# First and last groups of a two-layer graph network: statistics behind the adjacency transpose, split copies, row scalings and a tail on VectorE, and store deadlines taken from products

## The chip, the cores and the metric

The kernel runs on one core of a Trainium2 chip. Five instruction queues work side by side: TensorE (PE) for matrix products, VectorE (DVE), ScalarE (ACT), GpSimd (POOL), and SyncE (SP), which only issues DMAs here. The metric is device microseconds of one execution. The time is a median of three runs; one further execution was profiled.

## The reference

There are 128 batches, each of 128 tokens of width 512. Layer 0 mixes the tokens with the 128 x 128 adjacency matrix, adds the result to its input and normalises; layer 1 is masked attention with 8 heads of width 64, a projection, an inner layer norm, the residual and an outer layer norm.

```python
def layer0(x):                            # W1 = W2 = adj
    A = einsum('od,bdn->bon', adj, x); C = A + b[None, :, None]
    pre = A[:, :, None, :] + (C - A)[:, :, :, None]
    return layernorm(x + max(relu(pre), axis=-1))      # no gamma, no beta
def layer1(x):
    q, k, v = heads(x @ w_qkv)
    attn = softmax(where(mask == 0, -inf, q k^T * hd**-0.5))
    o = (attn @ v) @ w_proj + b_proj
    ln = layernorm(o) * gamma + beta
    return layernorm(x + o + ln)
```

The mask is built from `adj`. The maximum over the last axis needs only a row maximum of `A` and the bias, so layer 0 is one product with `adj` for each batch, a row maximum, and a norm.

## The kernel before

**Staging.** The 128 batches go in 32 groups of G = 4. All arithmetic is float32. Loop step `p` of the main part works on several groups at once: attention output of group p-1 (`attend`), scores and softmax of group p (`scores`, `softmax`), values of group p (`v_unit`), the layer-0 product of group p+2 (`l0_mm`) and its norm and transposition (`group_l0`), output projection of group p-1 (`o_unit`), queries and keys of group p+1 (`token_sums`, `qk_unit`), and the final norms and stores of group p-1 (`tails`). A prologue does layer 0 of groups 0 and 1 and the queries and keys of group 0 (`qk_plain`); an epilogue handles the last two groups batch by batch (`tail_pool`, `seed_last`, `project`, `tail_open`, `tail_close`, `outer`).

**Softmax** (L1020). For a batch, DVE adds the mask to the scores out of PSUM (`s<-k,mask`), takes row maxima (`nm<-s`), ACT makes eight exponentials with sums (L1054), DVE the reciprocals (`rec<-sm`), ACT scales the eight heads by them (L1071), and DVE transposes in 32 x 32 blocks (`pu<-s`, L1083). A pair of DMAs (`hop<-pu`, `s<-hop`) finishes the transposition through DRAM.

**Queries and keys** (`qk_unit`, L739). A fast-multiplication scheme has 26 nodes. A node is one or more products into a PSUM bank `k`; POOL's `hl` sums are their left sides. From some nodes ACT copies the bank to another bank that continues it (`seeds`, shown as `ACT k L773`) or to a snapshot in SBUF (`ACT u L777`). Two nodes in each group need a snapshot added to their bank by DVE before they go on (`k<-k,u`, L340): first node 7, then node 11. ACT then copies the second sum to `u`, and PE continues in that bank. The results leave through DVE (`qk<-k,u`).

**Final norms** (`tails`, L1155). For each half of a batch pair DVE runs two `scalar_tensor_tensor` operations through the helper at L343: `z<-o,mvo,ga_bc`, (o - mean) x gamma, and `z<-z,rs,o`, z x root + o. POOL adds the residual `xr`, ACT norms (L501), SP stores.

**Who sets the order.** The program calls `plan.add` with engine, cost, reads and writes. PE operations form a chain in program order. `Plan.schedule` (L217) lists all others: each operation gets a due time from its successors, and of those ready on an engine the most pressing goes first. Operations without successors, mainly stores, take a common due time at the end of everything:

```python
end = max(ideal[op] + op.cost for op in ideal) + 9.0
due = min((s.due - ... for s in op.succs), default=end)
```

`Plan.run` (L194) repeats this with shifted PE start times, four times (`ROUNDS`), and keeps the order that ends first. Each engine then executes its instructions in the order so found. Helpers record all operations of a kind, so many instructions have one line: L340 two-input elementwise, L343 `scalar_tensor_tensor`, L346 products, L350 DMAs.

**Prologue, lines that matter.** `l0_stats` (L516) calls `bn` (L457) for four batches; `finish` (L462) makes root and shift on POOL; `l0_transpose_pe` (L567) transposes on PE and copies 128x512 with one DVE instruction (L583); PE's order is l0 products for batches 0 to 3, transposes, `qk_plain(0)`, transposes, four `l0_mm`, `qk_plain(1)`.

**Epilogue, lines that matter.** For a batch of group 30, `tail_pool` (L1348) does inner statistics, a POOL finish of three small operations, an ACT norm, three POOL two-input operations (x gamma, + o, + residual) and `outer`. For a batch of group 31 `tail_open` (L1386) and `tail_close` (L1406) add the residual to the projection with an identity product on PE and read it from PSUM with a DVE `scalar_tensor_tensor`.

Of the kernel before, what the change touches and what calls it, by code (L numbers as in the profile page):

```python
# [135 lines left out]
class Op:  # L136
    __slots__ = ("n", "eng", "cost", "emit", "lag", "kb", "preds", "succs", "due", "start", "done")
# [22 lines left out]
class Plan:  # L160
# [5 lines left out]
    def add(self, eng, cost, emit, reads=(), writes=(), lag=None, kb=0):  # L166
        op = Op(len(self.ops), eng, cost, emit, self.LAG[eng] if lag is None else lag, kb)
        for accesses, writing in ((reads, False), (writes, True)):
            for a in accesses:
                buf, key = a if type(a) is tuple else (a, None)  # L170
                assert self.slots[buf.slot] is buf, buf.slot
                for other, k, w in buf.log:
                    if (w or writing) and (k is None or key is None or k == key):
                        op.preds.add(other)
                if buf.before is not None and (writing or not buf.log):
                    op.preds.update(o for o, _, _ in buf.before.log)
                buf.log.append((op, key, writing))
        if eng == "PE":
            if self.pe is not None:
                op.preds.add(self.pe)  # L180
            self.pe = op
        op.preds.discard(op)
        self.ops.append(op)
        return op
# [6 lines left out]
    ROUNDS, KEPT = 4, 0.5  # L191
    SLOWER, LATER = 1.05, 2.0

    def run(self, lead):  # L194
        for op in self.ops:
            for p in op.preds:
                p.succs.append(op)
        t = lead
        start = {}
        for op in self.ops:  # L200
            if op.eng == "PE":
                start[op] = t
                t += op.cost
        best = None
        for _ in range(self.ROUNDS):
            order = self.schedule(start)
            last = max(op.done for op in start)
            if best is None or last < best[0]:
                best = last, order
            t = was = lead  # L210
            for op in start:
                t += self.KEPT * (op.start - was)
                was, start[op] = op.done, t
                t += op.cost
        return best[1]

    def schedule(self, ideal):  # L217
        ops = self.ops
        end = max(ideal[op] + op.cost for op in ideal) + 9.0
        for op in reversed(ops):  # L220
            ahead = op.lag + (self.AHEAD_DMA + 1.5 * op.kb / self.KB_PER_US if op.kb else self.AHEAD)
            due = min(
                (s.due - (0.0 if s.eng == op.eng == "PE" else ahead) for s in op.succs),
                default=end,
            )
            if op in ideal:
                due = min(due, ideal[op] + op.cost)
            op.due = due - op.cost
# [56 lines left out]
def kernel(  # L285
# [137 lines left out]
    plan.add("DVE", 0.25, lambda: pin(V.tensor_copy(adjT.t, pt0.t[:, :P])), [pt0], [adjT])  # L423
# [33 lines left out]
    def bn(src, reads, mv, c):  # L457
        st = small("st", 6)
        plan.add("DVE", 0.61, lambda: pin(V.bn_stats(st.t, src())), reads, [st])  # L459
        plan.add("DVE", 0.09, lambda: pin(V.bn_aggr(mv.t[:, c], st.t)), [st], [(mv, c)])  # L460
# [33 lines left out]

    def norm(dst, src, stat, reads, writes):
        rs, sh, i = stat
        plan.add(
            "ACT",
            0.7,
            lambda: pin(  # L500
                A.activation(  # L501
                    dst(), src(), AF.Identity, bias=sh.t[:, i : i + 1], scale=rs.t[:, i : i + 1]
                )
            ),
            [rs, sh, *reads],
            writes,
        )
# [8 lines left out]
    def l0_stats(g):  # L516
        mv = buf(f"mvy{g % 2}", [P, G, 2])
        for j in range(G):
            xb = xs[2 * g + j // 2]
            bn(lambda xb=xb, j=j: xb.t[:, j % 2], [(xb, j % 2)], mv, j)  # L520
        return mv
# [45 lines left out]
    def l0_transpose_pe(f, k):  # L567
# [5 lines left out]
        def emit():  # L573
            for c in range(KC):
# [4 lines left out]
        plan.add(  # L579
            "DVE",  # L580
            0.61,
            lambda: pin(
                V.tensor_copy(  # L583
                    xT.t[:, h, :, ts(j, P)], b.t.rearrange("p (c n) -> p c n", c=KC)
                )
            ),
            [b],
            [(xT, (h, j))],
        )
# [97 lines left out]
    def qk_plain(h, banks, eng):  # L687

        xT = x1T_buf(0)
        for n in range(4):  # L690
            b = bank(banks[n])
            for half in range(2):
# [11 lines left out]
                plan.add("PE", 1.725, emit, [raw[n], (xT, (h, 0)), (xT, (h, 1))], [b])  # L704
# [315 lines left out]
    def softmax(b, bs):  # L1020
# [45 lines left out]
        for i in range(H):  # L1066
            plan.add(
                "ACT",
                0.295,
                lambda i=i: pin(  # L1070
                    A.activation(  # L1071
                        flat()[:, i], flat()[:, i], AF.Identity, scale=rec.t[:, i : i + 1]
                    )
                ),
                [rec, (s, i)],
                [(s, i)],
            )
        u = buf(f"pu{b % 2}", [P, Q, H, QS])
# [132 lines left out]
    for c in range(4):  # L1211
        (s,) = finish(mv0, [c], rcol[0])
        l0_norm_one(0, c, s)
# [4 lines left out]
    qk_plain(0, (0, 1, 2, 3), ("ACT", "DVE", "ACT", "DVE"))  # L1218
    for f in range(2, 4):
        l0_transpose_pe(f, 4 + f)  # L1220
    for f, k in zip(range(4, 8), (0, 1, 2, 3)):
        l0_mm(f, k)
# [4 lines left out]
    qk_plain(1, (4, 5, 6, 7), ("ACT", "DVE", "ACT", "DVE"))  # L1227
# [25 lines left out]
    for p in range(NG - 1):  # L1253
# [9 lines left out]
        for j in range(G):  # L1263
            softmax(a + j, bs[j])
# [48 lines left out]
    for j in range(G):  # L1313
        softmax(a + j, bs[j])
# [33 lines left out]
    def tail_pool(b, o, j):  # L1348
# [4 lines left out]
        (st,) = finish(mv, range(1))  # L1353
        norm(z, lambda: o.t[:, j], st, [o], [zk])
        for with_, op, rd in (
            (lambda: ga_bc.t, ALU.mult, ga_bc),
            (lambda: o.t[:, j], ALU.add, o),
            (r, ALU.add, rk),
        ):
            plan.add(  # L1360
                "POOL", 1.25, lambda with_=with_, op=op: tt(GP, z(), z(), with_(), op), [zk, rd], [zk]
            )
# [23 lines left out]
    def tail_open(b, pb):  # L1386
# [3 lines left out]
        rs = small("rs", G)  # L1390

        def root():
            pin(GP.tensor_scalar(rs.t[:, :1], mv.t[:, 0:1, 1], EPS, None, ALU.add))
            tt(GP, rs.t[:, :1], rs.t[:, :1], mhalf.t, ALU.pow)

        plan.add("POOL", 0.8, root, [mv, mhalf], [rs])
# [9 lines left out]
    def tail_close(b, pb, rs):  # L1406
# [3 lines left out]
        plan.add("PE", 0.862, lambda: mm(pb.t, ident.t, r(), False), [rk, ident], [pb])  # L1410
        plan.add(
            "DVE",
            0.65,
            lambda: stt(z(), z(), rs.t[:, :1], pb.t, ALU.mult, ALU.add),
            [zk, pb, rs],
# [8 lines left out]
    for j in range(G):  # L1424
        tail_pool(a - G + j, os_[g - 1, j // 2], j % 2)
    project(a, pbs[0])
    attend(a + 2, Y[0])
    opened = [tail_open(a, pbs[0])]
    project(a + 1, pbs[1])
    attend(a + 3, Y[1])  # L1430
    opened.append(tail_open(a + 1, pbs[1]))
    tail_close(a, pbs[0], opened[0])
    project(a + 2, pbs[2])
    opened.append(tail_open(a + 2, pbs[2]))
# [49 lines left out]
```

## Time and profile before

| what | value |
|---|---|
| median of 3 runs | 1915.88 us (1914.39 to 1916.46) |
| the profiled execution | 1916.16 us; its span 1914.4 us, so 1.76 us lie around the span |
| mean granted TensorE clock | 0.994 |
| busy PE / DVE / ACT / POOL | 98% / 81% / 73% / 70% |
| PE instructions' idle time put down to releasers, all waits | 18.8 us in 17 waits |
| PE busy from 0 to 50 / 50 to 100 us | 45.96 / 45.06 us |
| PE busy from 100 to 1840 us | 1733.57 of 1740 us |
| PE busy from 1840 to 1900 / 1900 to 1915 us | 51.80 / 0.00 us |

A row of the profile names engine, line and operation, then out<-in by the program's buffer names. Brackets at a timeline row give the idle time just before the instruction on its engine and what released it. PE's end times are modelled, so its busy share is an upper figure. The table says where PE isn't busy: the first 100 us, the last 75 us, and a little in between.

### The profile page before, as it was taken

Reading aid. Unit: us, or ns where it says so; the run is one execution under the profiler, and the core shown is the slowest. Engines: PE = TensorE matmul, PEld = TensorE weight load, DVE = VectorE, ACT = ScalarE, POOL = GpSimd, SP = SyncE. Lnnn points to the kernel's source line nnn. Section 1 sums busy time; section 2 is a strip of 40 time slices with the busy share of each in tenths; the row PEclk is TensorE's granted clock in tenths of the full one; section 3 lists DMA queues with packets and bytes.
Section 4 is the critical chain, followed back from the end, with each engine's and each line's share of the span. In section 5 each row is a group of like instructions: output and inputs, shape, how many; then the busy total and the mean of one; then the engine's idle time right before and its main releaser. Section 6 shows DMA issues by size and latency. Waiting matters only on the chain.

```text
span 1914.4 us, 35277 instructions
## 1 busy us (share of the span) xinstructions
PE 1876.4 (98%) x11307; PEld 1595.4 (83%) x11307; DVE 1558.2 (81%) x2634; ACT 1405.4 (73%) x4285; POOL 1332.8 (70%) x1454
## 2 busy tenths in 40 slices
PE   9899999999999999999999999999999999999995
PEld 6788888888888888888888888888888888888882
DVE  7678878889788878888788888888788887888774
ACT  2776778777778777778777787776788767787784
POOL 7658667667577767777677767686776776777746
PEclk9999999999999999999999999999999999999998
DMA  6656675566766566765576756676765667666653
GB/s 204 183 130 155 184 204 162 171 168 193 204 188 168 172 179 187 210 178 167 164 194 179 211 164 172 169 200 186 211 144 172 179 188 210 178 170 171 165 193 116
DMA packets 444856, 341.89 MB, mean 179 GB/s; under 512 B 276736, under 2 KB 378240, under 8 KB 444672
## 3 DMA queue, kind: packets, MB, share of 16 engines
q1 hardware_dynamic: 444384, 339.11, 63.7%
q8 instruction: 91, 1.49, 0.3%
q14 instruction: 93, 0.76, 0.1%
q10 hardware_dynamic: 288, 0.52, 0.1%
HBM read 172.82 MB, written 166.72 MB: 177 GB/s over the span
## 4 chain that ended last, share of the span: by engine, by line
PE 91%; DVE 3%; ACT 3%; POOL 1%; issue 1%; DMA 0%; ACTq 0%; DVEq 0%; POOLq 0%
PE k L346 91%; DVE z L343 2%; ACT s L1071 1%; ACT s L1054 1%; POOL x L340 1%; DVE wqk L340 0%; ACT u L777 0%; DVE k L340 0%; POOL rs L340 0%; ACT k L773 0%; DMA x<-in_x_dram 0%; DVE qk L343 0%; ACT x L501 0%; DVE st L459 0%; DVE x1T L583 0%
## 5 line engine op out<-in xcount | busy, mean ns | idle before, releaser
L346 PE MATMUL k<-hl,wqk 128*128 128x256 f32 x2232 | 518.9, 380 | 2.1 <-ACT k L773 2.0
L346 PEld LDWEIGHTS k<-hl,wqk 128*128 128x128 f32 x2232 | 424.4, 190 | 61.2 <-POOL hl L340 2.5
L1054 ACT ACTIVATE s<-s,nm 128x128 f32<-128x128 f32 x1024 | 397.2, 391 | 31.2 <-DVE nm L1045 31.2
L340 POOL TENSOR_TENSOR hl<-x1T 128x512 f32<-128x512 f32 (+1 forms) x250 | 237.8, 961 | 134.3 <-PE k L346 90.2
L1071 ACT ACTIVATE s<-s,rec 128x128 f32<-128x128 f32 x1024 | 325.5, 392 | 0.0
L346 PE MATMUL k<-x1T,wqk 128*128 128x256 f32 x992 | 250.0, 383 | 9.1 <-ACT u L777 5.6
L886 ACT COPY u<-k 128x512 f32<-128x512 f32 x189 | 110.0, 582 | 196.1 <-PE k L346 195.4
L777 ACT COPY u<-k 128x512 f32<-128x512 f32 x341 | 194.2, 584 | 73.2 <-DVE k L340 30.6
L346 PE MATMUL k<-wv,hl 128*128 128x256 f32 x1024 | 241.4, 379 | 0.0
L346 PEld LDWEIGHTS k<-wv,hl 128*128 128x128 f32 x1024 | 194.5, 190 | 52.1 <-issue 21.5
L346 PE MATMUL k<-wp,so 128*128 128x256 f32 x992 | 224.8, 379 | 0.5 <-ACT k L861 0.5
L343 DVE SCALAR_TENSOR_TENSOR s<-k,mask 128x512 f32<-128x512 f32 x256 | 156.2, 683 | 83.0 <-PE k L346 83.0
L346 PEld LDWEIGHTS k<-x1T,wqk 128*128 128x128 f32 x992 | 188.3, 191 | 40.6 <-ACT u L777 11.4
L343 DVE SCALAR_TENSOR_TENSOR qk<-k,u 128x512 f32<-128x512 f32 x248 | 165.4, 682 | 62.9 <-PE k L346 39.9
L346 PEld LDWEIGHTS k<-wp,so 128*128 128x128 f32 x992 | 188.4, 190 | 26.6 <-ACT k L861 0.9
L340 POOL TENSOR_TENSOR hl<-x1T,hl 128x512 f32<-128x512 f32 (+1 forms) x249 | 201.9, 822 | 0.5 <-DMA x1T<-xhop 0.5
L1054 ACT ACTIVATION_READ_ACCUMULATOR s<-s,nm 128x1 f32 x1024 | 194.2, 190 | 0.0
L346 PE MATMUL k<-wv,x1T 128*128 128x256 f32 x768 | 179.5, 383 | 0.0
L340 POOL TENSOR_TENSOR x<-x,be_bc 128x1024 f32<-128x1024 f32 x62 | 153.2, 2470 | 35.1 <-ACT xr L501 16.4
L346 PE MATMUL k<-wp,oT 128*128 128x256 f32 x744 | 170.7, 379 | 0.0
L1083 DVE STREAM_TRANSPOSE pu<-s 128x1024 f32<-128x1024 f32 x128 | 158.1, 1235 | 12.1 <-ACT s L1071 12.0
L1132 ACT COPY oT<-k 128x512 f32<-128x512 f32 x128 | 74.9, 585 | 120.3 <-PE k L346 120.3
(139 smaller groups left out, 3345.1 us busy)
## 6 DMA issues: line engine op xcount, KB each, us to landing
hop<-pu SPq DMA_DIRECT2D x128, 512.0 KB, 2.7
s<-hop SPq DMA_DIRECT2D x512, 128.0 KB, 3.7
spill<-x SPq DMA_DIRECT2D x62, 512.0 KB, 4.3
xhop<-xt SPq DMA_DIRECT2D x248, 128.0 KB, 3.4
x1T<-xhop SPq DMA_DIRECT2D x248, 128.0 KB, 5.0
x<-in_x_dram SPq DMA_DIRECT2D x60, 512.0 KB, 5.9
xr<-spill SPq DMA_DIRECT2D x60, 512.0 KB, 5.4
out_dram<-xr SPq DMA_DIRECT2D x60, 512.0 KB, 4.4
```

Source lines behind the costliest of these rows:

```text
L340: pin(eng.tensor_tensor(dst, a, b, op))
L343: pin(V.scalar_tensor_tensor(dst, a, s, b, op0, op1))
L346: pin(PE.matmul(dst, lhsT=lhsT, rhs=rhs, start=start, stop=True, skip_group_check=True))
L777: plan.add("ACT", 0.5, lambda b=b, u=u: pin(A.copy(u.t, b.t)), [b], [u])
L886: plan.add("ACT", 0.5, lambda: pin(A.copy(u.t, b.t)), [b], [u])
L1054: A.activation(flat()[:, i], flat()[:, i], AF.Exp, bias=nm.t[:, i : i + 1], accum_out=sm.t[:, i : i + 1],)
L1071: A.activation(flat()[:, i], flat()[:, i], AF.Identity, scale=rec.t[:, i : i + 1])
L1083: V.transpose(u.t.rearrange("p q h b -> p h q b"), flat().rearrange("p h (q a) -> p h q a", q=Q),)
L1132: lambda: pin(A.copy(dst.t[:, :, ts(jj, P)], bk.t.rearrange("p (c n) -> p c n", c=KC))),
```

## The change

1. **Statistics of group 0** are placed behind the copy of the transposed adjacency (`behind=[adj_done]`).
2. **`finish_first`**: for group 0, the shift is made by two small DVE operations; POOL keeps only the root.
3. **Split copies**: the 128x512 copy out of the PE transpose becomes two halves, the first on DVE, the second on ACT, and each half of a `qk_plain` product waits for its halves alone.
4. **Order on PE**: l0 products of batches 6 and 7 go between the second and third output block of `qk_plain(1)`.
5. **`softmax(on_vector)`**: for the four batches of group 0 and the first two of group 31, the eight ACT scalings become one DVE multiplication, 128x1024, with the reciprocals broadcast.
6. **Epilogue**: `tail_pool` becomes `tail_before`, called batch by batch between the attention and projection steps: the ACT norm and two of the three POOL operations become two DVE `scalar_tensor_tensor`s. `tail_close` loses its identity product; DVE adds the projection to the residual in SBUF and then combines. The shift of these inner norms is no longer needed, and `root_only` makes the roots.
7. **Planner**: an operation without successors takes its due time from the start of the PE operation that was the latest when it was added, plus 9.0 (`BEHIND`); six rounds instead of four; the starts of the best order are kept with it. PE's order in the main loop isn't touched by this, but the orders of DVE, ACT, POOL and SP are.

```diff
-    def add(self, eng, cost, emit, reads=(), writes=(), lag=None, kb=0):
+    def add(self, eng, cost, emit, reads=(), writes=(), lag=None, kb=0, behind=()):
         op = Op(len(self.ops), eng, cost, emit, self.LAG[eng] if lag is None else lag, kb)
+        op.after = self.pe
+        op.preds.update(behind)
...
-    ROUNDS, KEPT = 4, 0.5
+    ROUNDS, KEPT, BEHIND = 6, 0.5, 9.0
...
-                best = last, order
+                best = last, order, [op.start for op in order]
...
-        end = max(ideal[op] + op.cost for op in ideal) + 9.0
...
-            due = min(
-                (s.due - (0.0 if s.eng == op.eng == "PE" else ahead) for s in op.succs),
-                default=end,
-            )
+            if op.succs:
+                due = min(s.due - (0.0 if s.eng == op.eng == "PE" else ahead) for s in op.succs)
+            else:
+                due = ideal.get(op.after, 0.0) + self.BEHIND
...
+    def finish_first(mv, c, rows):
...
+        plan.add("POOL", 0.85, root, [(mv, c), mhalf], [rs])
+        plan.add("DVE", 0.12, lambda: tt(V, t..., mean, rows, ALU.add), ...)
+        plan.add("DVE", 0.12, lambda: stt(sh..., rows, t, rs, ALU.subtract, ALU.mult), ...)
...
-            bn(lambda xb=xb, j=j: xb.t[:, j % 2], [(xb, j % 2)], mv, j)
+            bn(lambda xb=xb, j=j: xb.t[:, j % 2], [(xb, j % 2)], mv, j, [adj_done])
...
+            if half:
+                plan.add("ACT", 0.4, lambda ops=operands: pin(A.copy(*ops())), [b], at)
+            else:
+                plan.add("DVE", 0.4, lambda ops=operands: pin(V.tensor_copy(*ops())), [b], at)
...
+        if on_vector:
             plan.add(
-                "ACT",
-                0.295,
...
+                "DVE",
+                1.55,
+                lambda: tt(
+                    V, flat(), flat(), rec.t.unsqueeze(2).to_broadcast([P, H, P]), ALU.mult
+                ),
...
-    for f, k in zip(range(4, 8), (0, 1, 2, 3)):
-        l0_mm(f, k)
+    for f in (4, 5):
+        l0_mm(f, f - 4)
...
-    qk_plain(1, (4, 5, 6, 7), ("ACT", "DVE", "ACT", "DVE"))
+    qk_plain(1, (4, 5, 6, 7), copies, range(2))
+    for f in (6, 7):
+        l0_mm(f, f - 4)
+    qk_plain(1, (4, 5, 6, 7), copies, range(2, 4))
...
-            softmax(a + j, bs[j])
+            softmax(a + j, bs[j], p == 0)
...
-        softmax(a + j, bs[j])
+        softmax(a + j, bs[j], j < 2)
...
-        (st,) = finish(mv, range(1))
-        norm(z, lambda: o.t[:, j], st, [o], [zk])
-        for with_, op, rd in (
-            (lambda: ga_bc.t, ALU.mult, ga_bc),
-            (lambda: o.t[:, j], ALU.add, o),
-            (r, ALU.add, rk),
-        ):
+        rs = root_only(mv, range(1))
+        plan.add("DVE", 0.7, lambda: stt(z(), o.t[:, j], mv.t[:, 0, 0:1], ga_bc.t, ALU.subtract, ALU.mult), ...)
+        plan.add("DVE", 0.7, lambda: stt(z(), z(), rs.t[:, :1], o.t[:, j], ALU.mult, ALU.add), ...)
+        plan.add("POOL", 1.25, lambda: tt(GP, z(), z(), r(), ALU.add), [zk, rk], [zk])
...
-        plan.add("PE", 0.862, lambda: mm(pb.t, ident.t, r(), False), [rk, ident], [pb])
+        plan.add("DVE", 0.65, lambda: tt(V, r(), r(), pb.t, ALU.add), [pb, rk], [rk])
...
-            lambda: stt(z(), z(), rs.t[:, :1], pb.t, ALU.mult, ALU.add),
+            lambda: stt(z(), z(), rs.t[:, :1], r(), ALU.mult, ALU.add),
...
-    for j in range(G):
-        tail_pool(a - G + j, os_[g - 1, j // 2], j % 2)
+    tail_before(a - 4)
     project(a, pbs[0])
     attend(a + 2, Y[0])
+    tail_before(a - 3)
```

## The prediction

> **What bounds the kernel now.** I read the page's slices and chain first, then PE's waits, then the timeline where those waits lie.
>
> ```profile
> PE   9899999999999999999999999999999999999995
> ACT  2776778777778777778777787776788767787784
> ...
> PE 91%; DVE 3%; ACT 3%; POOL 1%; issue 1%; DMA 0%; ACTq 0%; DVEq 0%; POOLq 0%
> ```
>
> PE is the chain; only the first slices and the last fall short. So whatever adds PE idle time adds that time, and other engines count only where PE waits for them or after its end. PE's waits say where that is:
>
> ```profile
> PE k L346 <- ACT u L777: 5.6, 5, 1.1
> PE k L346 <- ACT k L773: 5.1, 3, 3.1
> PE k L346 <- DMA s<-hop: 1.5, 1, 1.5
> PE k L346 <- DVE u L355: 1.2, 1, 1.2
> PE k L346 <- DVE adjT L423: 1.0, 1, 1.0
> ...
> PE k L346 <- DVE x1T L583: 0.9, 1, 0.9
> PE k L346 <- DVE z L343: 0.9, 1, 0.9
> PE k L346 <- DVE qk L712: 0.9, 1, 0.9
> ```
>
> By windows, adjT, x1T and qk L712 are the prologue, ACT k L773 is 4.8 us in 50 to 100 us (loop step 0), ACT u L777 is five stalls spread over the middle, DMA s<-hop is the tail. PE's last product ends at 1895.8 of 1914.4 us: 18.6 us of tail follow it.
>
> Step 0 in the timeline, PE at the ends of its two waits for seed copies:
>
> ```profile
> 82.79 1.10 PE L346 MATMUL k<-hl,wqk 128*128 128x256 f32 x4 [1.76 <-ACT k L773]
> ...
> 86.34 0.57 ACT L773 COPY k<-k 128x512 f32<-128x512 f32 x1
> ...
> 86.96 2.08 PE L346 MATMUL k<-x1T,wqk 128*128 128x256 f32 x4 [3.07 <-ACT k L773]
> ...
> 88.83 1.91 PE L346 MATMUL k<-hl,wqk 128*128 128x256 f32 x4
> ```
>
> The seed copies stand in ACT's queue behind 32 exponentials and 32 scalings, and after the second wait four matmuls take 2.08 us instead of 1.03: with 1.91 for 1.03 and the next eight (2.91 for 1.89) that is 2.9 us more.
>
> A middle stall, one of five:
>
> ```profile
> 260.14 0.70 DVE L340 TENSOR_TENSOR k<-k,u 128x512 f32<-128x512 f32 x1 [0.55 <-PE k L346]
> 260.75 1.88 DVE L343 SCALAR_TENSOR_TENSOR z<-o,mvo,ga_bc 128x512 f32<-128x512 f32 x1
> ...
> 262.55 3.44 DVE L343 SCALAR_TENSOR_TENSOR z<-z,rs,o 128x512 f32<-128x512 f32 x2
> ...
> 265.91 0.69 DVE L340 TENSOR_TENSOR k<-k,u 128x512 f32<-128x512 f32 x1
> ...
> 267.27 1.13 PE L346 MATMUL k<-x1T,wqk 128*128 128x256 f32 x4 [1.12 <-ACT u L777]
> ```
>
> Three z operations lie between the group's two DVE adds. The adds start d = 5.77 us apart; ACT's copy and PE follow the second by 1.36 us. Groups with two z's have d = 4.06 to 4.64 and no stall: **the stall is d - 4.64**.
>
> [...] a z takes 0.70 us alone, 1.7 to 2.85 beside POOL's 128x512 and 128x1024 sums; z<-z,rs,o averages 1.28. [...] doubled matmuls after 3.07 us of waiting, and pairs of l0 products at 2.07 us early on against 1.02 later. [...]
>
> **The change part by part**, against the profiled 1916.16 us.
>
> *Prologue.* (a) With the statistics behind it, the adjT copy no longer waits for a bn_stats that ended at 5.91 us; the transpose ended at 4.31. Of the 1.0 us wait and 0.3 us before, 0.1 to 1.0 can pass on, since the statistics (4 x 0.69) come later and the norms of batches 0 and 1, which bind the first transposes, follow DVE's order: 0.5. [...] Two DVE shift operations for three POOL ones: nothing, beside l0 products. (b) qk_plain(1) starts at 35.64 after waits of 0.86 (DVE qk L712, for a bank) and 0.90 (x1T copies, 34.31 to 35.58, late in DVE's queue behind wqk sums of 1.5 us which POOL blocks). With l0_mm of 6 and 7 moved behind two output blocks, the bank wait has 7 us of cover, and a half copy is 0.35 us on DVE with the other on ACT: of 1.76 us about 1.1 goes, what stays is the first DVE half behind a wqk sum. The moved l0_mm (4 x 0.5 us of PE) are neither added nor removed; their row maxima and norms come 7 us later, ahead of group 1's work by far more. Together -1.6 (-0.6 to -2.1).
>
> *Step 0.* 32 scalings leave ACT (pitch 0.305 us: 9.8 us), more than both waits, 1.76 + 3.07 = 4.8; with them go 2.9 us of slow clock: 7.7. Four DVE multiplications 128x1024 come: [...] DVE is busy 30.5 of 50 us there[...]. Queued behind them are the transposes pu (1.25 us), a DMA hop and two v adds; PE waits for those up to 1 us: **-7** (-8 to -4).
>
> *Planner.* Stores are due earlier now, so the final norms and z's before them are placed earlier. The compiled order keeps PE's instructions of the middle, but between the two adds DVE now has three z's in 9 groups (steps 2, 6, 9, 12, 15, 17, 20, 23, 26), xt and three z's in 7 (7, 10, 13, 18, 21, 24, 27), one z in 8, against three z's in 5 groups and two in most others before. Sixteen stalls instead of five. A group with one z can't give back: PE has no wait there. Each stall is at least what the trace has for three z's, 1.12; I take 1.12 for all 16, because the xt (0.70, one input, not blocked) runs while [...]z would stand anyway: 16 x 1.12 - 5.6 = **+12.3**. Upper end: laid against POOL's sums as traced, d is 5.99 and 6.31, stalls 1.35 and 1.67: 9 x 1.35 + 7 x 1.67 - 5.6 = +18.2; with one more blocked z, d = 6.9, up to +29. Lower end: the sums start at other times and the z's pass between them: -5.6, no stall. SP's queue carries stores earlier and loads as before; its DMA share is 0.65, so I take nothing, 0 to +2 if a reload is passed.
>
> *Tail.* ACT loses 16 scalings (4.9 us) in the last softmax, for two DVE multiplications[...]; so the exponentials, transposes and the DMA pair that PE waited for (1.5) come about 4 us earlier; 4 identity products (4 x 0.5 us) go from PE. After PE's end the chain was POOL: 1.26 us operations up to 1897.3, then roots; the last norm ended at 1911.5 and the span 2.9 later. Eight of twelve POOL operations (8 x 1.25 = 10 us) go, for 8 DVE ones at 0.70; four PSUM adds (0.65)[...] come too. DVE has about 25 us of work from the first attend on, and ends some 56 us after the last scores start (1840.9); roots 1.9, two norms 1.5 and 2.9 to the end make 62, against 73.5: **-11** (-6 to -14). If DVE's operations are blocked by the POOL adds left, -6.
>
> Sum: -1.6 - 7 + 12.3 - 11 = -7.3, or 1908.9 against 1916.16. The profiled run lies 0.28 above the median, so 1908.6, called 1909.
>
> **The rivals.**
> *The middle takes no harm.* POOL starts with PE's products, and its order changes too; if the z's fall between its sums, d stays under 4.64. Against it: three z's never did that in the five groups that had them. Sum -1.6 - 7 - 11 - 5.6 + up to 5: 1891 to 1896, say 1895. Chance 0.19.
> *The middle eats the gain, slower.* One mechanism: z's blocked by POOL's sums between the two adds, in 16 groups. The gains are 19.6 and the old stalls 5.6; it decides where a stall averages over 25.2 / 16 = 1.58 us, d over 6.2. For it: 5.99 and 6.31 from traced rows, and a longest z of 2.85. Against: the old 5.77. At d = 6.9 (2.26 each) +30.6 - 19.6 = +11: 1927; at 6.4, +3.4. Chance 0.27.
> *The tail is DVE's.* -6 instead of -11, and step 0 gives -5: -1.6 - 5 - 6 + 12.3, about 1916. For it: DVE is the fullest engine there after PE. Chance 0.16.
> That the planner change leaves the middle alone is excluded by the compiled order.
>
> **How the numbers follow.** The forecast has 0.38. A measurement of this kernel tells about 0.2%, 3.8 us, from no change. Faster takes the forecast but for 0.02, and the first rival: 0.55. Within: 0.02, the tail's 0.15 and 0.02 of the slow case: 0.19. Slower: 0.26. The forecast's own range is 1902 to 1912; with the others' inner halves 1896 to 1923.
>
> **What would show it.** Right: first l0 product near 5 us; no wait over 0.5 us near 34 us; ACT k L773 waits below 1 us in 50 to 100 us and no doubled matmuls at 87; PE <- ACT u L777 some 16 times, 1.1 each; last norm some 11 us nearer to the last scores. The forecast is wrong if ACT u L777 stays under 6 us in all (then near 1895), or passes 25 (then slower), or if the POOL roots in the tail still end over 10 us after PE.

## The result: 0.4% slower

The changed kernel takes 1923.66 us (median of 6 runs, 1920.72 to 1924.34), the kernel before 1915.14 in the six that stand beside them. The ratio is 1.0041, 95% interval 1.0028 to 1.0054. The forecast was 1909, with a range of 1896 to 1923. The profiled execution took 1924.27 us with a span of 1922.5, against 1916.16 and 1914.4.

The page of the changed kernel, chain by engine:

```profile
PE 84%; DVE 7%; ACT 5%; issue 2%; POOL 1%; DMA 1%; ACTq 0%; SPq 0%; DVEq 0%
```

PE's share of the chain fell from 91% to 84%: some of the time of others is now on the path. PE's three largest waits, by what ended them (total us, times, longest; the change moves lines, so L346 of before is L349, L773 is L810 and L777 is L814):

```profile
PE k L349 <- ACT u L814: 23.0, 16, 1.7
PE k L349 <- DVE x1T L625: 4.4, 2, 3.3
PE k L349 <- ACT k L810: 2.3, 3, 1.2
```

Sixteen stalls on `u`, as many as forecast, but 23.0 us in all instead of 18. Of the 4.4 us for x1T, 1.1 is the wait at the first queries and keys, which was 0.9 before; the 3.3 are new. The seed copies cost 1.2 us in step 0 instead of 4.8.

To put the 8.1 us of span in their place I cut each trace where PE starts the scores of a group (the `k<-qk` rows of the timeline). "Step 0" goes from the first group's scores to the second's, "middle" from there to the last group's, "tail" from the last group's to the end of the span.

| us | to first scores | step 0 | middle | tail |
|---|---|---|---|---|
| before | 49.65 | 54.28 | 1736.93 | 73.51 |
| changed | 52.58 | 47.55 | 1755.95 | 66.41 |
| difference | +2.9 | -6.7 | +19.0 | -7.1 |
| forecast | -1.6 | -7 | +12.3 | -11 |

**The middle.** The timeline of one of the seven groups with xt and three z's between the adds:

```profile
490.29 0.70 DVE L343 TENSOR_TENSOR k<-k,u 128x512 f32<-128x512 f32 x1 [1.05 <-ACT k L810]
490.89 0.70 DVE L570 STREAM_TRANSPOSE xt<-x 128x512 f32<-128x512 f32 x1
...
491.52 0.71 DVE L346 SCALAR_TENSOR_TENSOR z<-o,mvo,ga_bc 128x512 f32<-128x512 f32 x1
...
491.68 2.77 POOL L343 TENSOR_TENSOR x<-x,be_bc 128x1024 f32<-128x1024 f32 x1 [0.51 <-DVE xt L570]
492.14 4.53 DVE L346 SCALAR_TENSOR_TENSOR z<-z,rs,o 128x512 f32<-128x512 f32 x2
...
494.41 1.71 POOL L343 TENSOR_TENSOR hl<-x1T 128x512 f32<-128x512 f32 x1
...
496.09 1.71 POOL L343 TENSOR_TENSOR hl<-x1T,hl 128x512 f32<-128x512 f32 x1
...
496.60 0.69 DVE L343 TENSOR_TENSOR k<-k,u 128x512 f32<-128x512 f32 x1
...
497.95 0.48 PE L349 MATMUL k<-x1T,wqk 128*128 128x256 f32 x1 [1.73 <-ACT u L814]
```

The adds start 6.31 us apart. Two z's take 4.53 us, where two alone take 1.4: the first of them stands until POOL's 128x1024 sum is done, and the next again beside an hl sum. POOL's 128x1024 sum itself waited for xt. The second add, which has one of its inputs in PSUM, takes its usual 0.69 us beside the next hl sum; of the 62 such adds in this trace none takes over 0.70.

**The prologue.** POOL and DVE from 30 us on, then PE:

```profile
30.36 2.51 POOL L343 TENSOR_TENSOR x<-x,be_bc 128x1024 f32<-128x1024 f32 x1
30.60 2.55 DVE L343 TENSOR_TENSOR wqk<-xr 128x256 f32<-128x256 f32 x1
...
33.08 0.74 DVE L625 COPY x1T<-k 128x256 f32<-128x256 f32 x2
```

```profile
28.68 1.88 PE L349 MATMUL k<-o,adjT 128*128 128x512 f32 x4
33.87 10.15 PE L349 MATMUL k<-x1T,oT 128*128 128x256 f32 x32 [3.31 <-DVE x1T L625]
...
45.58 7.07 PE L349 MATMUL k<-x1T,so 128*128 128x256 f32 x32
```

PE came to the second half of the first queries and keys at 30.5 us and waited 3.31 us for DVE's half copies, which stood behind a weight sum that POOL blocked (2.55 us for an operation that takes 0.41 alone). Then 32 matmuls took 10.15 us; the like 32 at 45.58 took 7.07. The granted clock was 0.50 from 33.1 to 39.9 us and 1.00 from 40 on: the wait brought the half clock with it, 3.0 us more.

**Step 0.** PE at its wait for the seed copies:

```profile
85.10 1.10 PE L349 MATMUL k<-hl,wqk 128*128 128x256 f32 x4 [1.18 <-ACT k L810]
86.04 1.03 PE L349 MATMUL k<-x1T,wqk 128*128 128x256 f32 x4
```

One wait of 1.18 us instead of two that made 4.8, and no doubled matmuls after it; before, the granted clock was 0.50 from 85.8 to 92.6 us. **The tail** is shown with its experiment below.

### The profile page after: what moved, and what is told of

Same layout as the page of the kernel before. It is cut to its first block, busy times and chain, and to the rows that moved or that the text cites. A ratio compares the mean times of both kernels' runs of the same rounds, so it can differ in the third digit from the quotient of the medians.

```text
span 1922.5 us, 35153 instructions
## 1 busy us (share of the span) xinstructions
PE 1871.2 (97%) x11299; PEld 1593.2 (83%) x11299; DVE 1571.2 (82%) x2660; ACT 1394.0 (73%) x4237; POOL 1337.2 (70%) x1426
## 4 chain that ended last, share of the span: by engine, by line
PE 84%; DVE 7%; ACT 5%; issue 2%; POOL 1%; DMA 1%; ACTq 0%; SPq 0%; DVEq 0%
PE k L349 84%; DVE z L346 4%; ACT s L1119 1%; ACT k L810 1%; ACT s L1091 1%; DVE k L343 1%; DVE wqk L343 1%; ACT u L814 1%; ACT x L535 1%; DMA hop<-pu 0%; POOL rs L343 0%; DVE xt L570 0%; DVE st L462 0%; DVE pu L1131 0%; ACT u L923 0%
## 5 line engine op out<-in xcount | busy, mean ns | idle before, releaser
L349 PE MATMUL k<-hl,wqk 128*128 128x256 f32 x2232 | 517.9, 379 | 1.7 <-ACT k L810 1.4
L349 PEld LDWEIGHTS k<-hl,wqk 128*128 128x128 f32 x2232 | 423.7, 190 | 60.6 <-POOL hl L343 2.2
L343 POOL TENSOR_TENSOR hl<-x1T 128x512 f32<-128x512 f32 (+1 forms) x250 | 249.7, 1009 | 101.4 <-PE k L349 70.5
L1119 ACT ACTIVATE s<-s,rec 128x128 f32<-128x128 f32 x976 | 308.3, 392 | 0.0
L349 PE MATMUL k<-x1T,wqk 128*128 128x256 f32 x992 | 249.1, 381 | 24.0 <-ACT u L814 23.0
L814 ACT COPY u<-k 128x512 f32<-128x512 f32 x341 | 193.5, 583 | 100.8 <-PE k L349 45.4
L346 DVE SCALAR_TENSOR_TENSOR s<-k,mask 128x512 f32<-128x512 f32 x256 | 158.7, 681 | 105.9 <-PE k L349 105.9
L349 PE MATMUL k<-wv,hl 128*128 128x256 f32 x1024 | 241.4, 379 | 0.0
L349 PEld LDWEIGHTS k<-wv,hl 128*128 128x128 f32 x1024 | 194.5, 190 | 52.1 <-issue 22.2
L349 PEld LDWEIGHTS k<-x1T,wqk 128*128 128x128 f32 x992 | 187.0, 190 | 55.9 <-ACT u L814 29.9
L349 PE MATMUL k<-wp,so 128*128 128x256 f32 x992 | 224.5, 379 | 0.0
L346 DVE SCALAR_TENSOR_TENSOR qk<-k,u 128x512 f32<-128x512 f32 x248 | 168.8, 685 | 67.2 <-PE k L349 47.2
L343 POOL TENSOR_TENSOR hl<-x1T,hl 128x512 f32<-128x512 f32 (+1 forms) x249 | 214.2, 873 | 0.2
L349 PEld LDWEIGHTS k<-wp,so 128*128 128x128 f32 x992 | 188.4, 190 | 25.7 <-issue 0.2
L349 PE MATMUL k<-wv,x1T 128*128 128x256 f32 x768 | 179.5, 383 | 0.0
L1131 DVE STREAM_TRANSPOSE pu<-s 128x1024 f32<-128x1024 f32 x128 | 157.7, 1232 | 20.3 <-ACT s L1119 19.6
L349 PE MATMUL k<-wp,oT 128*128 128x256 f32 x744 | 170.7, 379 | 0.0
```

Source lines behind the costliest of these rows:

```text
L343: pin(eng.tensor_tensor(dst, a, b, op))
L346: pin(V.scalar_tensor_tensor(dst, a, s, b, op0, op1))
L349: pin(PE.matmul(dst, lhsT=lhsT, rhs=rhs, start=start, stop=True, skip_group_check=True))
L814: plan.add("ACT", 0.5, lambda b=b, u=u: pin(A.copy(u.t, b.t)), [b], [u])
L1119: A.activation(flat()[:, i], flat()[:, i], AF.Identity, scale=rec.t[:, i : i + 1])
L1131: V.transpose(u.t.rearrange("p q h b -> p h q b"), flat().rearrange("p h (q a) -> p h q a", q=Q),)
```

## The experiments

All stage times below are from one profiled execution of each kernel.

| us | to first scores | step 0 | middle | tail | time |
|---|---|---|---|---|---|
| deadlines_back | 52.44 | 47.55 | 1757.19 | 68.53 | 1926.30 |
| z_behind_add | 51.97 | 47.57 | 1729.40 | 68.78 | 1899.84 |
| z_one_input | 52.27 | 47.56 | 1727.85 | 66.42 | 1895.87 |
| tail_back | 46.66 | 51.05 | 1781.59 | 71.42 | 1953.35 |
| zb_x1t_on_act | 45.80 | 50.44 | 1730.94 | 68.80 | 1895.12 |
| zb_order_back | 45.76 | 49.87 | 1730.37 | 68.60 | 1896.38 |
| zb_tail_shift | 51.83 | 47.56 | 1729.79 | 65.75 | 1896.71 |
| zb_order_shift | 45.68 | 49.87 | 1730.37 | 65.67 | 1894.70 |
| before_tail | 46.84 | 54.88 | 1732.47 | 74.21 | 1910.18 |
| before_p0 | 47.49 | 47.99 | 1734.97 | 74.05 | 1906.29 |
| before_z_behind | 47.52 | 54.27 | 1728.35 | 73.71 | 1905.63 |
| deadlines_alone | 48.24 | 55.55 | 1741.53 | 72.56 | 1919.66 |

Times are medians of four runs for deadlines_back, z_behind_add, zb_x1t_on_act and zb_order_shift, and single runs for the others; the four runs of zb_x1t_on_act lie 4.2 us apart, so a difference of 1 or 2 us between single runs says nothing, and the stages carry the argument. The kernel before had medians of 1913.96 to 1915.79 beside them.

**Theories.** A: the place of the z operations between the two adds, together with POOL's sums beside them (a z takes 0.70 to 0.75 us away from these, up to 2.85 beside them), makes the middle longer, and the planner puts them there for reasons that have nothing to do with a wait, since it prices a z at 0.7 us. B, my prediction's: the new store deadlines put them there. By trace A can be counted: an undisturbed group lasts 57.67 us from scores to scores. In the changed kernel a group with "z<-o, z, z" lasts 59.15, one with "xt, z<-o, z, z" 59.66, one with "xt, z, z" 57.98.

### deadlines_back: deadlines and rounds of part 7 undone

```diff
-    ROUNDS, KEPT, BEHIND = 6, 0.5, 9.0
+    ROUNDS, KEPT = 4, 0.5
...
-            if op.succs:
-                due = min(...)
-            else:
-                due = ideal.get(op.after, 0.0) + self.BEHIND
+            due = min((...), default=end)
```

> The changed kernel with the planner's deadlines and rounds of before (part 7 undone), all else kept. Compiled, 9 groups have z<-o, z, z between the two adds, 8 have xt, z<-o, z, z and one has xt, z, z. Theory A (the place of the z's decides, whoever put them there; from the changed kernel's groups a 'z<-o, z, z' group lasts 1.48 us longer than an undisturbed one of 57.67, an 'xt, z<-o, z, z' one 1.99, an 'xt, z, z' one 0.32): middle 30 x 57.67 plus 9 x 1.48 + 8 x 1.99 + 0.32 = 29.6, so about 2 us more than the changed kernel, 1922 to 1927 in all. Theory B (the new deadlines made the stalls, as I predicted): the middle returns to about 1737 and the total to about 1905.

Middle 1757.19, time 1926.30; ratio to before 1.0065 (1.005 to 1.008). PE's waits on `u`:

```profile
PE k L350 <- ACT u L815: 25.1, 17, 2.1
```

Theory A's count holds within 1 us (1.2 over the changed kernel where 2 was expected), B is refuted: the old deadlines give the same stalls. In the kernel before, the same deadlines give three z's in five groups only; so something else in the change, through the planner, brings them.

### tail_back: part 6 undone

```diff
-    def tail_before(b):
+    def tail_pool(b, o, j):
...
-    tail_before(a - 4)
+    for j in range(G):
+        tail_pool(a - G + j, os_[g - 1, j // 2], j % 2)
```

(and `tail_open`, `tail_close` as before)

> The changed kernel with the epilogue of before (part 6 undone); nothing in the main loop is edited. Compiled, 26 groups have xt, z<-o, z, z between the adds. Theory A: middle 30 x 57.67 + 26 x 1.99, about 1780, which is 24 us over the changed kernel; the tail itself 66 to 72; total about 1950. Rival (the epilogue can't reach the middle; only what the loop contains counts): middle stays near 1756 and the total changes by the tail alone, to about 1928.

Middle 1781.59 where 1780 was expected, time 1953.35 where 1950 was:

```profile
PE k L349 <- ACT u L814: 46.3, 27, 1.7
```

Restoring an epilogue that runs in the last 75 us puts xt and three z's between the adds in 26 groups and makes the loop 25.6 us longer. Nothing in the loop's code is different. The z order is settled by a plan over the whole program, and an edit far away can move it.

### z_one_input: the z's without a second SBUF input

```diff
-    lambda ...: stt(z.t[:, j], o.t[:, j], mv.t[:, c, 0:1], ga_bc.t, ALU.subtract, ALU.mult)
+    lambda ...: pin(V.transpose(z.t[:, j], o.t[:, j]))
...
-    lambda ...: stt(z.t[:, j], z.t[:, j], rs.t[:, c : c + 1], o.t[:, j], ALU.mult, ALU.add)
+    lambda ...: pin(V.transpose(z.t[:, j], o.t[:, j]))
```

> The changed kernel with each z operation of the loop replaced by a DVE 32x32 block transposition of the same 128x512 size, one SBUF input instead of two, at the same planned cost and place; the inner norm's arithmetic is left out. Theory A[...]: each takes about 0.69 us, d is 2.8 to 3.5, no stall, middle about 1729. Rival (three operations are too many for DVE whatever they are, or POOL's sums are late by themselves): d stays over 4.6 and stalls over 0.5 us remain.

DVE, and POOL's 128x1024 sum, in the same group as above:

```profile
486.21 0.70 DVE L343 TENSOR_TENSOR k<-k,u 128x512 f32<-128x512 f32 x1 [1.05 <-ACT k L810]
486.82 0.70 DVE L570 STREAM_TRANSPOSE xt<-x 128x512 f32<-128x512 f32 x1
487.44 0.67 DVE L1222 STREAM_TRANSPOSE z<-o 128x512 f32<-128x512 f32 x1
487.60 2.37 POOL L343 TENSOR_TENSOR x<-x,be_bc 128x1024 f32<-128x1024 f32 x1 [0.51 <-DVE xt L570]
488.03 1.26 DVE L1229 STREAM_TRANSPOSE z<-o 128x512 f32<-128x512 f32 x2
489.66 0.70 DVE L343 TENSOR_TENSOR k<-k,u 128x512 f32<-128x512 f32 x1 [0.36 <-PE k L349]
```

The three operations in the same places now take 1.9 us, DVE even waits for PE before the second add, and all groups of the middle last 57.67 us, but the last (55.51, as in the changed kernel). So neither three instructions nor their order is enough for a stall. What the edit takes from the z's is the second SBUF input and their arithmetic; the two weren't tried apart. Two of the transpositions lie wholly beside POOL's sum and take 1.26 us together, and the sum takes 2.37 us and not 2.77. The changed kernel's trace has the same difference between DVE's operations: with one SBUF input, the 120 xt take 0.67 to 0.71 us and the 62 adds 0.66 to 0.70, 49 of these wholly beside POOL's work; with two, z<-z,rs,o takes 0.71 to 2.85.

### z_behind_add: the z's made to follow the second add

```diff
+                    second_add[g] = plan.add("DVE", 0.62, ...)          # k<-k,u; the later one stays
...
                     [(z, j)],
+                    behind=[second_add[g + 2]],                          # at both z operations
```

> The changed kernel with the z operations of a loop step made to follow the second add of that step's queries and keys. Theory A: no z is between the adds, d falls under 4.3, the 16 stalls go; middle about 1729 instead of 1756, total 1895 to 1900. Rival: the z's, now beside the qk outputs and the next mask additions, are late there and PE waits for those instead: middle over 1740, total over 1908.

```profile
PE k L349 <- DVE x1T L625: 4.6, 2, 3.3
PE k L349 <- ACT k L810: 3.3, 3, 1.7
PE k L349 <- ACT u L923: 2.6, 2, 1.3
```

No wait on L814 is left; middle 1729.40, time 1899.84. The ratio to before is 0.9925 (0.9909 to 0.9942): with this one edit the changed kernel is 14 us faster than before, not 8 slower. What the rival expected, PE held elsewhere, shows only in the last step of the middle (57.00 against 55.51) and in the tail (+2.4 us).

### before_z_behind: the same edit on the kernel before

```diff
+                    behind=[second_add[g + 2]],
```

> The kernel before with the z's behind the second add, nothing of the change. By the loss of d over 4.35 us, the kernel before has 5 x 1.39 + 7 x 0.32 = 9.2 us of it; all of that goes: middle 1736.9 to about 1729, total 1905 to 1908. Rival (only gaps that the wait list shows cost time, 5.6 us): middle about 1731.5 and total about 1909.

Middle 1728.35, time 1905.63. The gain of 8.6 us in the middle is more than the 5.6 that the list of waits showed. Groups with d = 4.63 lasted 57.99, 0.32 over the rest, with no idle time recorded; the loss of a group is about d - 4.35, not d - 4.64. One group (step 2) got longer, 59.41 instead of 57.81, by a new wait of 1.7 us for a mask addition, which stands behind two moved z's in DVE's queue; here they do cost something.

### deadlines_alone: deadlines and rounds of part 7 on the kernel before

```diff
+            else:
+                due = ideal.get(op.after, 0.0) + self.BEHIND
```

> The kernel before with the planner's part alone (part 7). The compiled loop has one z<-o, z, z and 13 xt, z, z between the adds. Theory A: middle about 1733, total 1909 to 1912. My prediction's step, that earlier store deadlines bring the stalls: middle at 1749 or more, total 1926.

The time is 1919.66, between the two. The middle is 1741.53; the stalls on `u` are 2.5 us in 3 times, so B's stalls don't come, but other waits grow: 7.7 us for a seed copy in step 0, and the DMA hop in the last groups:

```profile
PE k L346 <- ACT k L773: 10.1, 3, 7.7
PE k L346 <- DMA s<-hop: 4.5, 2, 3.0
PE k L346 <- ACT u L777: 2.5, 3, 1.1
```

The step from group 30's scores to group 31's lasts 58.61 against 54.74. That earlier deadlines do this by themselves is one run's finding; its path was not followed.

### before_p0: step-0 scalings on DVE alone

```diff
-            softmax(a + j, bs[j])
+            softmax(a + j, bs[j], p == 0)
```

> The kernel before with the step-0 scalings on DVE alone. Step 0 was 54.28 before and 47.55 in the changed kernel; if that part does it alone, 47.5 to 49 here. The compiled loop has one z<-o, z, z and 13 xt, z, z between the adds: middle 57.67 x 30 + 1.39 + 13 x 0.32 and the little that groups 1 and 2 cost, about 1733. Total 1903 to 1906. Rival (step 0 got shorter only because PE came to it 3 us later in the changed kernel): step 0 at 51 or more.

Step 0 is 47.99: this part makes the gain alone, and the rival falls. The time is 1906.29.

None of the parts tried alone on the kernel before (5 in step 0 here, 6 in before_tail below, 7 in deadlines_alone) brings the stalls: in each, one group from step 1 to step 29 has three z's between the adds, step 3. So none of these alone is the cause; parts 1 to 4, and combinations, were not tried.

### zb_x1t_on_act and zb_order_back: the prologue

Both start from z_behind_add. The first puts the late half copies on ACT, the second undoes part 4.

```diff
-            if half:
+            if half or f >= 2:
                 plan.add("ACT", 0.4, lambda ops=operands: pin(A.copy(*ops())), [b], at)
```

```diff
-    for f in (4, 5):
+    for f in range(4, 8):
         l0_mm(f, f - 4)
...
-    qk_plain(1, (4, 5, 6, 7), copies, range(2))
-    for f in (6, 7):
-        l0_mm(f, f - 4)
-    qk_plain(1, (4, 5, 6, 7), copies, range(2, 4))
+    qk_plain(1, (4, 5, 6, 7), copies, range(4))
```

> The kernel with z's behind the second add, and both half copies of the second pair of prologue transposes on ACT instead of one on DVE. Theory (the first DVE half stands in DVE's queue behind weight sums that POOL's weight sums block; PE waits 3.3 us for it and then runs at half clock for 3.0): the start of the first scores goes from 51.97 to about 45.7 us, total about 1893.5. Rival (DVE's next copy, qk out of PSUM, stands behind the same sums and holds PE's bank a little later, or ACT is late too): half of it at most, first scores at 48 to 50.

> The kernel with z's behind the second add, and the four layer-0 products of batches 4 to 7 together ahead of the second half of the first queries and keys, as before (part 4 undone). Same theory: PE has 1.9 us more to do before it needs the copy, so it waits about 1.4 instead of 3.3 and the clock isn't halved: first scores at about 47. Rival (the reordering isn't what exposes the wait): first scores stay at 52, or the bank wait comes back as well and they start later.

PE of zb_x1t_on_act:

```profile
28.46 1.88 PE L349 MATMUL k<-o,adjT 128*128 128x512 f32 x4
30.18 7.07 PE L349 MATMUL k<-x1T,oT 128*128 128x256 f32 x32
```

Wait and half clock are both gone (the granted clock is 1.00 from 25 to 50 us), and the first scores come 6.2 us sooner, where 6.3 were expected. That these agree is in part luck: in z_behind_add the 32 matmuls after the wait took 8.86 us, not 10.15, so wait and half clock made 5.3 us there; the other 0.9 was gained ahead of them, since the four products before the wait start at 28.46 us here and at 29.37 there. The time is 1895.12 (ratio 0.9897, 0.9881 to 0.9914). But step 0 gives 2.9 us back (50.44): first scores plus step 0 come to 96.2 here, 95.6 in zb_order_back, 95.5 in before_p0. PE's waits in step 0 differ: 2.2 us for ACT's seed copy here, the same and 1.5 for a POOL hl sum in zb_order_back, the hl sum alone in before_p0. Whether something common sets the end of step 0 near 95.5 was not tried.

With part 4 undone, PE doesn't wait for the copies at all. This doesn't single out PE's order, since DVE's changed with it: the copies start at 30.76 and not 33.76, with one weight sum fewer ahead of them, and PE comes to its products 1.3 us earlier. tail_back tells the two apart. It has PE's order of part 4 and the same 14 weight sums ahead of the copies, but of the last five sums three are blocked there, for 1.5 us each, and in the changed kernel all five, for up to 2.55:

```profile
28.73 1.48 DVE L343 TENSOR_TENSOR wqk<-xr 128x256 f32<-128x256 f32 x1
30.13 0.74 DVE L625 COPY x1T<-k 128x256 f32<-128x256 f32 x2
```

The last weight sum is through before POOL's 128x1024 sum starts (30.76), PE goes on at 30.93 without a wait, and the first scores start at 46.66. So part 4 takes away PE's cover, but the 3.31 us come from where DVE's weight sums fall beside POOL's.

### before_tail and zb_tail_shift: the epilogue

before_tail has part 6 on the kernel before. zb_tail_shift starts from z_behind_add and makes the shifts of the last norms on DVE:

```diff
-        (st,) = finish(mz, range(1))
-        norm(z, z, st, [zk], [zk])
+        rs, sh = root_only(mz, range(1)), small("sh", G)
+        plan.add("DVE", 0.2, lambda: stt(sh..., mean, -1.0, rs, ALU.mult, ALU.mult), [mz, rs], [sh])
+        norm(z, z, (rs, sh, 0), [zk], [zk])
```

> The kernel before with the new epilogue alone (part 6). The compiled loop has one group with z<-o, z, z between the adds and 9 with xt, z, z, so the middle should be 1731 to 1733 instead of 1736.9. If the parts of the tail add (the changed kernel's epilogue with part 6 undone took 71.4 instead of 66.4), the tail goes from 73.5 to 68.5 and the total to about 1906. Rival (the new epilogue gains only where the last softmax is off ACT): tail about 72, total about 1910.

> The kernel with z's behind the second add, and the shift of each last norm of the epilogue made by one small DVE operation instead of two on POOL. Theory (after the last products POOL's queue of small root and shift operations sets the end, about 6.5 us, of which the shifts are about 1.9): the tail, from the last scores to the end, goes from 68.8 to about 67. Rival (DVE's blocked additions set it): 68.8 or more, since DVE has more to do.

In before_tail the tail is 74.21: the new epilogue gains nothing alone, and my expectation that the parts add was wrong. Old epilogue and ACT scalings 73.5, old epilogue and DVE scalings 71.4 (tail_back), new epilogue and ACT scalings 74.2, both new 66.4: the gain needs both. The deadlines differ too (old in the first and third), but with the old ones both new parts still make 68.5 (deadlines_back). POOL at the end of the changed kernel shows what is left:

```profile
1911.62 0.21 POOL L1197 TENSOR_SCALAR rs<-mvl 128x1 f32<-128x1 f32 x1
1911.92 0.57 POOL L343 TENSOR_TENSOR rs<-rs,mhalf 128x1 f32<-128x1 f32 x1
...
1917.50 0.41 POOL L482 TENSOR_SCALAR sh<-mvm 128x1 f32<-128x1 f32 x2
1917.87 0.33 POOL L343 TENSOR_TENSOR sh<-sh,rs 128x1 f32<-128x1 f32 x2
```

At 1911.6 DVE has only the last batch's combination and statistics left (until 1914.2, and the combination waits 0.97 us for POOL's root). From there POOL works off roots and shifts of one column each for 6.6 us, and the last ACT norms start at 1918.09. Taking only the shifts away gives 3.0 us (68.78 to 65.75), where 1.9 were expected.

### zb_order_shift: the edits together

The edits of z_behind_add, zb_order_back and zb_tail_shift in one kernel.

> The changed kernel with three edits: z's behind the second add, the layer-0 products of batches 4 to 7 together as before, shifts of the last norms on DVE. If the stages add: 45.8 to the first scores, 49.9 for step 0, 1730.4 for the middle, 65.8 for the tail, span 1891.9, total about 1893. Rival (the planner, given the third edit, places the z's or the prologue's copies elsewhere): a stage off by more than 1.5 us.

The stages add to within 0.2 us (45.68, 49.87, 1730.37, 65.67). The time is 1894.70, where 1893 was expected; ratio to before 0.9895 (0.9878 to 0.9911): 1.05% faster than before, 1.5% faster than the change as made.

## Why the prediction was wrong, step by step

Between the forecast -7.3 and the measured +8.1 us of span lie 15.4: 6.7 in the middle, 4.5 in the prologue, 3.9 in the tail, 0.3 in step 0.

**Middle, +12.3 forecast, +19.0 measured: the mechanism and the groups were right, the term was mis-sized.** Nine and seven groups stall, for the reason given. The step that failed is "I take 1.12 for all 16", with the xt beside POOL's sum, where z would stand anyway. That xt itself isn't blocked holds: the 120 of before take 0.66 to 0.71 us, nine of them wholly beside POOL's work. But the trace has the order the other way round: POOL's 128x1024 sum starts when xt is done, so xt is not hidden under it but in front of it. The trace of before showed this already, in its seven groups of xt and two z's, step 4 for one:

```profile
319.88 0.70 DVE L536 STREAM_TRANSPOSE xt<-x 128x512 f32<-128x512 f32 x1
...
320.66 2.77 POOL L340 TENSOR_TENSOR x<-x,be_bc 128x1024 f32<-128x1024 f32 x1 [0.18 <-DVE xt L536]
```

The recorded stalls are 1.21 and 1.73, near the 1.35 and 1.67 that I had laid out and put aside as the upper end. With them the middle was +18.2, and the sum was -1.4 and not -7.3. The "stall is d - 4.64" also missed 0.3 us in each group, which the waits don't show and the length of the groups does: 9 x 1.48 + 7 x 1.99 + 0.31 = 27.6, less 5 x 1.39 + 7 x 0.32 = 9.2 before, makes 18.4; the last step's 0.8 does most of the rest. (The prediction's +29 for d = 6.9 should be the +30.6 that its second rival has.) **Its cause was wrong too.** I put the z's down to the deadlines; deadlines_back refutes it, and tail_back shows that an edit far from the loop does as much. Of parts 5 (in step 0), 6 and 7 none brings them alone on the kernel before; which part or combination does stays open.

**Prologue, -1.6 forecast, +2.9 measured: sign wrong.** The failed step is (b), "of 1.76 us about 1.1 goes, what stays is the first DVE half behind a wqk sum". The 1.76 was too much to begin with: the 0.90 of it is idle time of the weight load before 35.64, and PE itself has no recorded wait there (its 0.9 for x1T is at 16.05). A half copy takes 0.41 us on DVE, not 0.35. The two rows of before:

```profile
34.44 1.13 PE L346 MATMUL k<-o,adjT 128*128 128x512 f32 x2 [0.86 <-DVE qk L712]
35.64 7.17 PE L346 MATMUL k<-x1T,oT 128*128 128x256 f32 x32
```

From the first of the eight layer-0 products to 35.64 it is 4.80 us, and 3.76 in zb_order_back, which has no wait there: about 1.0 could be gained. And the time of the half copies is set by the 14 weight sums ahead of them in DVE's queue and by POOL's operations beside these (0.94 to 2.55 us for each of the last five, where such a sum takes 0.41 alone), not by PE. Moving two products behind took away 1.9 us of PE's work that had covered this. I counted the bank wait's new cover and not the copy wait's lost one: 3.31 us, and 3.0 of half clock after it. Step (a) was right in that the first layer-0 products start at 4.96 us. It gains nothing further on: in before_tail, where the early pairs of products took 1.02 to 1.12 us (1.02 to 1.45 in the changed kernel), the first queries and keys start at 13.78, in the changed kernel at 13.89. And 49.65 itself is high: before_z_behind, whose first 60 DVE instructions are the same as before's, comes to its first scores at 47.52, with the first pair of layer-0 products at 1.12 us and not 2.07 and the second at 1.02 and not 1.92. Against that the prologue is 5 us worse.

**Step 0, -7 forecast, -6.7 measured: right**, and before_p0 shows that part 5 does it. The DVE multiplications took 1.18 to 1.34 us, which no trace had shown beforehand; one seed-copy wait of 1.18 us stayed, where less than 1 was expected.

**Tail, -11 forecast, -7.1 measured: the term "roots 1.9" was mis-sized.** DVE's work was done but for one batch 55.5 us after the last scores, where I had 56. From there POOL's single-column operations took 6.6 us, the last batch's wait for its root among them, in place of the 1.9 worked out; that is about the whole miss. The sign set for it, POOL's roots ending over 10 us after PE, came true (1918.2 against 1903.7). I had counted the large POOL operations that go and not the small ones that queue behind one another when several batches come due together.

**The slower rival had the right mechanism and the right outcome, but the middle alone doesn't make the outcome.** I gave it 0.27; its d of 5.99 and 6.31 measured 5.86 and 6.31. It called the kernel slower where a stall averages over 1.58 us, and by group lengths the mean is 27.2 / 16 = 1.70. But by the same lengths the old stalls cost 9.2 us and not 5.6, which moves the limit to (19.6 + 9.2) / 16 = 1.80. With prologue, step 0 and tail as forecast, -19.6, the middle's +19.0 would have left the time as it was; the misses in prologue and tail, 8.4 us, made it slower. (Its figure at d = 6.4 should be +3.0, not +3.4.) The sign set for slower, over 25 us of waits on `u`, wasn't reached either: the list has 23.0, the lengths 27.2.

## What to carry to other kernels

Where a planner with fixed prices orders an engine's queue over a whole program, read the new order of the loop after any edit, however far away, and price it from the trace: DVE's z operations, with two inputs in SBUF, took up to 2.85 us here beside POOL's sums, planned at 0.7 and measured at 0.70 to 0.75 away from them. A single precedence edge that keeps such operations out of the stretch where PE waits was worth 24 us here, more than any part of the change gained. And when work is moved away from in front of a wait, ask which other wait it had covered.

## What was not expected of the hardware

PE's list of waits understates a stall by 0.26 to 0.32 us: groups with a recorded wait of 1.21 and 1.73 last 1.48 and 1.99 longer, and those with d = 4.63 last 0.32 longer with none recorded. The time from first to first of the same products in each group shows it. Set product by product beside an undisturbed group, the one with 1.73 has its first product after the wait start 1.90 us late, since the recorded end of the product before lies past the usual start of the next, and that first product takes 0.48 us and not 0.38. The groups with d = 4.63 have a gap of 0.05 us there, too short for the list, and lose 0.21 and 0.10 in the same two ways.

A wait of 3.31 us on PE cost another 3.0 by the half clock after it (10.15 us for 32 matmuls instead of 7.07 to 7.17, with a granted clock of 0.50 up to 39.9 us), so the wait was worth nearly double. How much follows isn't fixed: after 3.30 us of the same wait z_behind_add lost 1.7 (8.86 us for the 32), and its clock was granted at half for 3.4 us, in the changed kernel for 6.8. Slow matmuls came after a shorter wait too. In zb_x1t_on_act, after one of 2.21 us, four took 1.82 us where 1.03 is usual:

```profile
79.52 1.10 PE L349 MATMUL k<-hl,wqk 128*128 128x256 f32 x4 [2.21 <-ACT k L810]
80.46 1.82 PE L349 MATMUL k<-x1T,wqk 128*128 128x256 f32 x4
```

In zb_order_back none came after the same wait of 2.2 us (1.03 for the like four matmuls).

The start of the program, too, differed between the profiles of before and before_z_behind, which begin with the same instructions, by about 2 us at the first scores (49.65 and 47.52), 1.85 of it in two pairs of products that took 2.07 and 1.92 us instead of 1.12 and 1.02.
